# A two-layer convolution kernel: image 0's statistics partly on VectorE, ten extra matmuls at the start, and the fronts of images 1 and 2 begun two and three stages later

## The chip, the cores and the metric

The kernel runs on one core of a Trainium2 chip. The core has five engines with a queue each, worked off in order: PE (TensorE, matmuls), DVE (VectorE), ACT (ScalarE), POOL (GpSimd) and SP (SyncE, which here only issues DMAs; POOL issues DMAs too). 16 DMA engines move data between HBM and the on-chip memory SBUF; matmul results land in the accumulation memory PSUM. The metric is the device time of one execution in microseconds.

## The reference

The input x has 32 images of 256 channels and 32 x 32 pixels. Two residual layers are computed, with `_gn` a normalization over 32 groups of 8 channels:

```
x = x + L0(_gn(x));   x = x + L1(_gn(x))
L0: a = unfold(x, 3, 3); out = fq(fq(a) @ fq(weight.T)) + bias      # fq: round to 5 exponent, 10 mantissa bits
L1: y = relu(bn(w1 @ x))                                            # 256 -> 64 channels
    w = w2 @ y + b2                                                 # per pixel: 16 groups x 49 taps
    out[g, c, h, w] = sum over 49 taps k of w[g, k, h, w] * patch[g, c, k, h, w]
```

Layer 0 is a 3 x 3 convolution in float16; layer 1 is an involution: each pixel makes its own 7 x 7 filter for each of 16 groups.

## The kernel before

The 32 images go through a software pipeline. `tc.manual_schedule()` means that the written order is the order on every engine's queue. One loop runs over stages `n` from FRONT = -56 to the end; each image has 16 stages (`per`), and the main part of image b, its tap sums, starts at stage 16 b. Image b's front begins 56 stages ahead of that, so that some three and a half images are in work at a time. In a stage the loop first advances every open front by one step (each front is a generator; a `yield` ends its step), oldest image first, then issues tap sums, additions, `weights`, scatters, loads.

A front does, for one image (lines of the profile):

- statistics of layer 0: two sums of 1024 values a partition on ACT (L214, the `junk` output is thrown away, the sum is accumulated), a reduction over groups on DVE (`across`, `total`, `back`, L224 to L230), the `mean` on ACT (L235), two sums of squares on ACT (L214), the group reduction again, then `s` (square root, L245), `ve` (L247), the reciprocal `r` on DVE (L251), and `finish` on ACT: `t`, `w`, `u`, `rstd`, `off` (L256 to L267), eight small operations;
- `xq`, the normalized image in float16, by two ACT operations (L273). There is one `xq` for all images;
- the convolution: four units of 18 matmuls (`pc`, L332; 9 for each half of the input channels). After each unit DVE clamps it into `q` (L346) and adds it to x (L348), and ACT sums the new x for layer 1 (L214). Image 0 uses two PSUM buffers in turn, later images one, so the next unit waits for `q`. The units are cut into steps of 9 matmuls, 0, 9 and 0;
- the same statistics for layer 1, then `xn`, the normalized image reordered, by four ACT operations of 512 values (L273), `py` on PE (L377), `y` by two ACT operations (L388), and four times a transposition `pt` on PE (L396) with a copy to `pixels` on ACT (L400).

`weights` (eight times an image) computes the per-pixel filters on PE (`pw`, 32 matmuls, L411), and DVE adds the bias while it writes them to `w_sb` (`evict`, L435). `scatter` writes `w_sb` to HBM (`wd`, on SP, L476): a quarter of an image after its third, fifth, seventh and eighth `weights`. `load_bands` reads them back as bands (L497, 14 DMAs on POOL and 2 on SP), and `sums` multiplies bands with `pixels` on PE (`acc`, L522), which `add_windows` adds to x (L538) and `store` writes out (L543).

At the start the weights of layer 0 are loaded in two halves and clamped to float16 by `quantize_weights` on DVE (`wq`, L195), at stages FRONT + 2 and FRONT + 6.

Of the kernel before, what the change touches and what calls it, by code (L numbers as in the profile page):

```python
# [9 lines left out]
F32 = mybir.dt.float32  # L10
AF = mybir.ActivationFunctionType
ALU = mybir.AluOpType

P = 128
B, C, H, W = 32, 256, 32, 32
N = H * W
NT = 512
RT = NT // W
CH = C // P
# [6 lines left out]
GN = 8  # L26
SQ = 32
GN_EPS = 1e-5
# [44 lines left out]
FRONT = -56  # L73
LOAD = -63
LEAD = 18


@with_exitstack
def tile_quant_conv_then_involution(
# [10 lines left out]
    nc = tc.nc  # L90
# [4 lines left out]
    small = ctx.enter_context(tc.tile_pool(name="small", bufs=2))  # L95
# [5 lines left out]
    ps_m = ctx.enter_context(tc.tile_pool(name="ps_m", bufs=1, space=PSUM))  # L101

    def load_x(b):
        xt = xpool.tile([P, CH, N], F32, tag="x", name=f"x_{b}")
        for h in range(CH):
            nc.sync.dma_start(xt[:, h], x[b, h * P : (h + 1) * P])
        return xt
# [46 lines left out]
    wq = const.tile([P, CH, K0 * K0, C], F16, name="wq")  # L154
# [26 lines left out]
    for col, cols, at, n in (  # L181
# [4 lines left out]
        to = bass.AP(  # L186
            tensor=wd.tensor,
            offset=wd.offset + col * WPIX + at,
            ap=[[ROW, H], [WPIX, cols], [1, n]],
        )  # L190
        nc.sync.dma_start(to, bands[NBAND - 1][:H, 0, :n].unsqueeze(1).to_broadcast([H, cols, n]))

    def quantize_weights(kh):

        nc.vector.tensor_scalar(wq[:, kh], staged[kh], F16_MAX, -F16_MAX, ALU.min, ALU.max)  # L195
        nc.gpsimd.memset(bands[kh], 0.0)
        if kh == CH - 1:
            nc.gpsimd.memset(w_sb, 0.0)

    class GroupNorm:  # L200


        def __init__(self, b, layer):
            self.tiles = list(sums_sb[b % 2][layer])

        def begin(self, parts):
# [4 lines left out]
        def add_up(self, src, part, h, n0, n1, func, bias=0.0):  # L211
            junk = work.tile([P, N], F16, tag="junk", name="junk", bufs=1)
            i = part * CH + h
            nc.scalar.activation(  # L214
                junk[:, n0:n1], src[:, h, n0:n1], func, bias=bias, accum_out=self.sums[:, i : i + 1]
            )

        def group(self):


            if self.parts == 2:
                nc.vector.tensor_add(self.sums[:, :CH], self.sums[:, :CH], self.sums[:, CH : 2 * CH])
            across = small.tile([P, SQ], F32, tag="across", name="across")
            nc.vector.transpose(across, self.sums)  # L224
            total = small.tile([P, SQ // GN], F32, tag="total", name="total")
            nc.vector.tensor_reduce(
                total, across.rearrange("p (g r) -> p g r", r=GN), mybir.AxisListType.X, ALU.add
            )
            back = small.tile([P, SQ], F32, tag="back", name="back")
            nc.vector.transpose(back, total.unsqueeze(2).to_broadcast([P, SQ // GN, GN]))  # L230
            return back[:, :CH]
# [10 lines left out]
        def variances(self):  # L242
            pv = self.group()
            self.s = small.tile([P, CH], F32, tag="s", name="s")
            nc.scalar.activation(self.s, pv, AF.Sqrt, bias=eps, scale=1.0 / (GN * N))  # L245
            self.ve = small.tile([P, CH], F32, tag="ve", name="ve")
            nc.scalar.activation(self.ve, pv, AF.Identity, bias=eps, scale=1.0 / (GN * N))  # L247

        def scales(self):
# [3 lines left out]
        def finish(self):  # L253

            t = small.tile([P, CH], F32, tag="t", name="t")
            nc.scalar.activation(t, self.r, AF.Square)  # L256
            w = small.tile([P, CH], F32, tag="w", name="w")
            for h in range(CH):
                nc.scalar.mul(w[:, h : h + 1], t[:, h : h + 1], self.ve[:, h : h + 1])
            u = small.tile([P, CH], F32, tag="u", name="u")  # L260
            nc.scalar.activation(u, w, AF.Identity, bias=three_halves, scale=-0.5)
            self.rstd = small.tile([P, CH], F32, tag="rstd", name="rstd")
            self.off = small.tile([P, CH], F32, tag="off", name="off")
            for h in range(CH):
                one = slice(h, h + 1)
                nc.scalar.mul(self.rstd[:, one], u[:, one], self.r[:, one])
                nc.scalar.mul(self.off[:, one], self.m[:, one], self.rstd[:, one])  # L267
# [7 lines left out]
    LATER = 1  # L275

    def backwards(at):

        step, n = at.ap[-1]
        return bass.AP(tensor=at.tensor, offset=at.offset + step * (n - 1), ap=[*at.ap[:-1], [-step, n]])  # L280
# [3 lines left out]
    def front(b):  # L284


        xt = x_tiles[b]

        def stages(n):
            for _ in range(n):  # L290
                yield

        gn = GroupNorm(b, 0)
        gn.begin(1)
        for h in range(CH):
            gn.add_up(xt, 0, h, 0, N, AF.Identity)
            yield
        yield LATER
        gn.means()
# [12 lines left out]
        gn = GroupNorm(b, 1)  # L312
        gn.begin(N // NT)
        units = [(nt, mh) for nt in range(N // NT) for mh in range(CH)]
        for s in range(4 * len(units) + 2):
            u, i = divmod(s, 4)
            if u < len(units):
                nt, mh = units[u]
                if i == 0 and b == 0 and u % 2:

                    pc = ps_m.tile([P, NT], F32, tag="m", name="pc")
                elif i == 0:
                    pc = ps_c.tile([P, NT], F32, tag="pc", name="pc")
                for n in range(sum(CONV[:i]), sum(CONV[: i + 1])):
# [11 lines left out]
                        start=n == 0,  # L336
                        stop=n == CH * K0 * K0 - 1,
# [28 lines left out]
        for h in range(CH):  # L366
            yield
            to = xn[:, h].rearrange("p (k d r j) -> p d k r j", d=SIDES, r=TR, j=JC)
            at = xt[:, h].rearrange("p (k r d j) -> p d k r j", d=SIDES, r=TR, j=JC)
            gn.apply(h, [(to[:, 0], at[:, 0]), (to[:, 1], backwards(at[:, 1]))])  # L370
        yield from stages(2)

        py = ps_m.tile([P, NT], F32, tag="m", name="py")
        for kh in range(CH):
            px = xn[:, kh].rearrange("p (a i n) -> p a i n", i=2, n=2 * JC)
            for i in range(2):
# [4 lines left out]
                    start=kh == 0,  # L381
                    stop=kh == CH - 1,
                )
        to = y_sb[b % 2].rearrange("p (k r d j) -> p d k r j", k=K, d=SIDES, j=JC)
        of = py.rearrange("p (k d r j) -> p d k r j", k=K, d=SIDES, j=JC)
        for d in range(SIDES):
            at = of[:, d]
# [3 lines left out]
        for m in range(0, M, 2):  # L391
# [7 lines left out]
            to = pixels[(b * M + m) // 2 % NPIX].rearrange("p i a (v c) -> p (i a) v c", c=GC)  # L399
# [130 lines left out]
    def add_windows(b, m):  # L530

        d = m % SIDES
        to = x_tiles[b].rearrange("p h (r c) -> p h r c", c=W)
        j0 = d * (JC - PAD1)
        for g, at, top, f, l in windows(b, m):
            x_at = to[:, :, f:l, j0 : j0 + WINI]
            of = at.rearrange("p h j r -> p h r j")[:, :, f - top : l - top]
            nc.vector.tensor_tensor(x_at, of, x_at, ALU.add)  # L538

    def store(b, k):  # L540

        cols = slice(k * NT, (k + 1) * NT)
        nc.sync.dma_start(out[b].rearrange("(h p) n -> p h n", p=P)[:, :, cols], x_tiles[b][:, :, cols])  # L543
# [3 lines left out]
    per = 2 * M  # L547

    def due(n, lag):

        b, i = divmod(n - lag, per)
        return (b, i) if 0 <= b < B else (None, None)

    with tc.manual_schedule():
        fronts = {}
        for n in range(FRONT, B * per + 2):
            b, i = due(n, FRONT)
            if i == 0:
                fronts[b] = front(b)
            later = list(fronts)  # L560
            for part in range(2):
                for b in list(later):
                    got = next(fronts[b], fronts)
                    if got is fronts:
                        fronts.pop(b)
                    if got is not LATER:
                        later.remove(b)
            if n in (FRONT + CH, FRONT + CH + 4):
                quantize_weights((n - FRONT - CH) // 4)
            b, i = due(n, 0)  # L570
            if b is not None and i % 2 == 0:
                sums(b, i // 2)
            b, i = due(n, 1)
            if b is not None and i % 2 == 0:
                add_windows(b, i // 2)
                if i // 2 == M - 1:
                    store(b, 1)
                    x_tiles.pop(b)

            b, i = due(n, 2)  # L580
            if b is not None and i == 2 * (M - 1 - SIDES):
                store(b, 0)
            b, i = due(n, -LEAD)
            if b is not None and i % 2 == 0:
                weights(b, i // 2 * WR)

            for part in range(2):
                b, i = due(n, -LEAD + 1 + part)
                if b is not None and i % 2 == 0:
                    for k in range(K):  # L590
                        if i // 2 == min((k + 1) * TR // WR, H // WR - 1):
                            scatter(b, k, part)
            b, i = due(n, LOAD)
            if i == 0 and b > 1:
                x_tiles[b] = load_x(b)

            b, i = due(n, 3 - 4 * NBAND)
            if b is not None and i % 4 == 0:
                load_bands(b, i // 4)
# [38 lines left out]
```

## Time and profile before

| | |
|---|---|
| median of 3 runs | 1352.48 us (1352.35 to 1356.02) |
| the profiled execution | 1344.24 us, of which the span is 1342.5 us |
| mean granted TensorE clock | 0.982 |
| first matmul / first `py` / first `pw` | 15.24 / 50.66 / 55.66 us |
| first tap sum (`acc`) | 87.68 us |
| `py` of images 1, 2, 3, 4 | 78.53, 115.17, 155.22, 193.53 us |
| PE busy, 90 to 130 us | 40.0 of 40.0 us, DMA share 1.00 |

The profile gives, for each engine, its instructions with start, length, source line, output and inputs, and, in brackets, how long the engine was idle before and what ended that idle time. L332 is line 332 of the kernel before. `PEld` is the weight load of a matmul, which overlaps PE. "x18" at the end of a row is the number of instructions merged in it.

### The profile page before, as it was taken

What the parts mean: (1) busy time and instruction counts of PE and PEld (TensorE: products, weight loads), DVE (VectorE), ACT (ScalarE), POOL (GpSimd) and SP (SyncE); (2) the same over time, 40 slices, a digit from 0 to 9 for tenths busy, and PEclk for the clock granted to TensorE, in tenths of its full rate; (3) what the DMA queues carried; (4) which work ended last, traced back from release to release, by engine and by line L of the source; (5) the groups of instructions that cost most, each with busy time, mean ns of one, the idle gap of its engine ahead of it and who ended that gap; (6) DMA issues with size and microseconds to landing.
All of it is one profiled execution on the core that took longest, in us unless ns stands there. A gap on an engine that the chain in (4) does not pass through costs nothing.

```text
span 1342.5 us, 65799 instructions
## 1 busy us (share of the span) xinstructions
PE 1253.6 (93%) x27648; PEld 763.7 (57%) x27648; DVE 818.8 (61%) x2539; ACT 733.3 (55%) x1731; POOL 1014.4 (76%) x1818
## 2 busy tenths in 40 slices
PE   5899999999999999999999999999999999999665
PEld 2356566565555655556655556666555566556454
DVE  3466666565666665656665666766666666666442
ACT  5775656455656556556545655655556564553300
POOL 9067878777787778777778787788777877788785
PEclk9999999999999999999999999999999999999987
DMA  6089999999999999999999999999999999999995
GB/s 228 11 237 295 271 293 293 279 266 281 272 286 282 291 285 270 283 263 280 293 282 283 270 288 282 293 297 296 281 288 275 277 284 290 271 281 266 278 274 166
DMA packets 360724, 361.85 MB, mean 270 GB/s; under 512 B 75056, under 2 KB 304752, under 8 KB 359152
## 3 DMA queue, kind: packets, MB, share of 16 engines
q1 hardware_dynamic: 278512, 229.38, 56.8%
q0 software_dynamic: 81920, 128.28, 33.9%
q8 instruction: 220, 3.60, 1.1%
q14 instruction: 72, 0.59, 0.1%
HBM read 176.60 MB, written 180.76 MB: 266 GB/s over the span
## 4 chain that ended last, share of the span: by engine, by line
PE 60%; DMA 23%; POOL 7%; issue 3%; ACT 3%; DVE 2%; SPq 1%; POOLq 0%; DVEq 0%; ACTq 0%
PE pc L332 25%; PE acc L522 19%; DMA band<-wd 17%; PE pw L411 11%; POOL band L497 7%; DMA wd<-w_sb 6%; PE pt L396 3%; PE py L377 3%; ACT junk L214 1%; SPq L476 1%; DVE w_sb L435 1%; DMA x<-in_x 1%; ACT xn L273 0%; SPq L497 0%; ACT xq L273 0%
## 5 line engine op out<-in xcount | busy, mean ns | idle before, releaser
L497 POOL DMA_DIRECT2D band<-wd x1792 | 980.3, 549 | 315.7 <-DMA band<-wd 182.0
L435 DVE TENSOR_TENSOR w_sb<-pw,late_sb 128x224 f32<-128x224 f32 (+7 forms) x1280 | 330.4, 322 | 419.5 <-PE pw L411 419.2
L332 PE MATMUL pc<-xq,wq 128*128 128x496 f16 (+3 forms) x2304 | 535.2, 379 | 20.3 <-ACT xq L273 18.3
L522 PE MATMUL acc<-band,pixels 64*32 64x190 f32 (+1 forms) x16384 | 426.6, 332 | 51.8 <-DMA band<-wd 42.7
L522 PEld LDWEIGHTS acc<-band,pixels 64*32 64x32 f32 x16384 | 304.7, 107 | 159.7 <-issue 81.1
L332 PEld LDWEIGHTS <-wq 128*128 128x128 f16 x2304 | 206.7, 98 | 316.1 <-issue 102.7
L411 PE MATMUL pw<-late_sb,y 64*32 64x224 f32 (+1 forms) x8192 | 288.9, 333 | 10.8 <-issue 9.4
L538 DVE TENSOR_TENSOR x<-acc,x 128x380 f32<-128x380 f32 (+1 forms) x512 | 262.0, 512 | 32.2 <-PE acc L522 23.2
L411 PEld LDWEIGHTS pw<-late_sb,y 64*32 64x32 f32 x8192 | 186.5, 106 | 38.1 <-issue 21.0
L400 ACT COPY pixels<-pt 128x512 f32<-128x512 f32 x128 | 73.7, 576 | 228.6 <-PE pt L396 228.6
L214 ACT ACTIVATE junk<-x 128x512 f16<-128x512 f32 (+1 forms) x192 | 146.4, 763 | 14.7 <-DVE x L348 12.2
L214 ACT ACTIVATE junk<-x,mean 128x1024 f16<-128x1024 f32 x128 | 147.1, 1149 | 4.3
L245 ACT ACTIVATE s<-back,eps 128x2 f32<-128x2 f32 x64 | 18.9, 296 | 178.6 <-DVE back L230 178.6
L346 DVE TENSOR_SCALAR q<-pc 128x512 f16<-128x512 f32 x128 | 87.2, 681 | 17.6 <-PE pc L332 17.6
L273 ACT ACTIVATE xn<-x,off,rstd 128x512 f32<-128x512 f32 x128 | 96.2, 800 | 0.0
L348 DVE SCALAR_TENSOR_TENSOR x<-q,early_sb,x 128x512 f32<-128x512 f16 x128 | 94.2, 736 | 0.3
L396 PEld LDWEIGHTS pt<-ident,xn 128*128 128x128 f32 x512 | 63.9, 142 | 26.3 <-issue 2.5
L396 PE MATMUL pt<-ident,xn 128*128 128x128 f32 x512 | 78.0, 275 | 0.1
L273 ACT ACTIVATE xq<-x,off,rstd 128x1024 f16<-128x1024 f32 x64 | 75.7, 1227 | 0.0
L235 ACT ACTIVATE mean<-back 128x2 f32<-128x2 f32 x64 | 12.6, 196 | 101.4 <-DVE back L230 101.4
L377 PE MATMUL py<-xn,early_sb 128*64 128x512 f32 x256 | 62.2, 606 | 0.9 <-ACT xn L273 0.9
L224 DVE STREAM_TRANSPOSE across<-sums 128x32 f32<-128x32 f32 x128 | 26.3, 205 | 33.6 <-ACT junk L214 32.4
(40 smaller groups left out, 369.3 us busy)
## 6 DMA issues: line engine op xcount, KB each, us to landing
wd<-w_sb SPq DMA_DIRECT2D x896, 160.0 KB
band<-wd POOLq DMA_DIRECT2D x1664, 70.5 KB, 4.6
x<-in_x SPq DMA_DIRECT2D x64, 512.0 KB
out<-x SPq DMA_DIRECT2D x64, 512.0 KB
band<-wd POOLq DMA_DIRECT2D x128, 60.5 KB, 4.6
band<-wd SPq DMA_DIRECT2D x128, 50.5 KB
band<-wd SPq DMA_DIRECT2D x128, 40.5 KB
band<-in_w SPq DMA_DIRECT2D x2, 1152.0 KB
```

Of the source, the lines that this page charges most:

```text
L214: nc.scalar.activation(junk[:, n0:n1], src[:, h, n0:n1], func, bias=bias, accum_out=self.sums[:, i : i + 1])
L273: nc.scalar.activation(dst, src, AF.Identity, bias=self.off[:, one], scale=self.rstd[:, one])
L332: nc.tensor.matmul(pc.rearrange("p (r c) -> p r c", c=W)[:, r0 - nt * RT : r1 - nt * RT, c0:c1], wq[:, kh, k, mh * P : (mh + 1) * P], xq[: ...
L346: nc.vector.tensor_scalar(q, pc, F16_MAX, -F16_MAX, ALU.min, ALU.max)
L348: nc.vector.scalar_tensor_tensor(xt[:, mh, cols], q, bias_sb[:, mh : mh + 1], xt[:, mh, cols], ALU.add, ALU.add)
L377: nc.tensor.matmul(py[i * CR : (i + 1) * CR], w1_sb[:, kh, :], px[:, :, i], start=kh == 0, stop=kh == CH - 1,)
L396: nc.tensor.transpose(pt[:, i, h * P : (h + 1) * P], xn[:, h, (m + i) * P : (m + i + 1) * P], ident)
L411: nc.tensor.matmul(pws[i][t * TW : (t + 1) * TW, : dj.stop - dj.start, r], y_sb[b % 2][half, (r0 // 2 + r) * W : (r0 // 2 + r + 1) * W], w ...
L435: nc.vector.tensor_tensor(to, of[:, :, d0:d1], bias[:, :, d0:d1], ALU.add)
L497: queue.dma_start(to, src)
L522: nc.tensor.matmul(at[t * TW : (t + 1) * TW, h, :, f - top : l - top], px[p, a, v * GC : v * GC + TW], of[:, :, a, f - top : l - top, v], ...
L538: nc.vector.tensor_tensor(x_at, of, x_at, ALU.add)
```

## The change

Four things are edited.

- Image 0's statistics: the second half's sum of layer 0 is a DVE reduction; in both layers `ve` and `finish` of image 0 are small DVE operations on both halves at once (five after the reciprocal, in place of eight on ACT). Of image 0's four `xn` operations two go to DVE.
- Ten matmuls of 512 columns on the first half of the clamped weights are issued right after that half is clamped; their result is not used. The second half is clamped at stage FRONT + 7 in place of FRONT + 6.
- The front of image 1 is held for its first two stages, that of image 2 for its first three (`HELD`).
- From its stage 16 on (`CATCH`), every second stage, a held front gets one additional step, two times for image 1 and three times for image 2, so that it is level with the others again before the tap sums of image 0 begin.

```diff
+WARM = 10
+HELD = {1: 2, 2: 3}
+CATCH = 16

+    def warm_up():
+
+        pc = ps_m.tile([P, NT], F32, tag="m", name="warm_pc")
+        for _ in range(WARM):
+            nc.tensor.matmul(pc, wq[:, 0, 0, :P], wq[:, 0, 1:3], start=True, stop=True)

         def __init__(self, b, layer):
+            self.first = b == 0

+        def add_up_by_vector(self, src, h):
+            nc.vector.tensor_reduce(self.sums[:, h : h + 1], src[:, h], mybir.AxisListType.X, ALU.add)

             self.ve = small.tile([P, CH], F32, tag="ve", name="ve")
+            if self.first:
+                nc.vector.tensor_scalar(self.ve, pv, 1.0 / (GN * N), GN_EPS, ALU.mult, ALU.add)
+                return
             nc.scalar.activation(self.ve, pv, AF.Identity, bias=eps, scale=1.0 / (GN * N))

             t = small.tile([P, CH], F32, tag="t", name="t")
+            if self.first:
+                self.rstd = small.tile([P, CH], F32, tag="rstd", name="rstd")
+                self.off = small.tile([P, CH], F32, tag="off", name="off")
+                nc.vector.tensor_mul(t, self.r, self.r)
+                nc.vector.tensor_mul(t, t, self.ve)
+                nc.vector.tensor_scalar(t, t, -0.5, 1.5, ALU.mult, ALU.add)
+                nc.vector.tensor_mul(self.rstd, t, self.r)
+                nc.vector.tensor_mul(self.off, self.m, self.rstd)
+                return
             nc.scalar.activation(t, self.r, AF.Square)

         for h in range(CH):
-            gn.add_up(xt, 0, h, 0, N, AF.Identity)
+            if b == 0 and h:
+                gn.add_up_by_vector(xt, h)
+            else:
+                gn.add_up(xt, 0, h, 0, N, AF.Identity)
             yield

-            gn.apply(h, [(to[:, 0], at[:, 0]), (to[:, 1], backwards(at[:, 1]))])
+            if b == 0:
+                one = slice(h, h + 1)
+                nc.vector.tensor_scalar(
+                    to[:, 0], at[:, 0], gn.rstd[:, one], gn.off[:, one], ALU.mult, ALU.add
+                )
+            else:
+                gn.apply(h, [(to[:, 0], at[:, 0])])
+            gn.apply(h, [(to[:, 1], backwards(at[:, 1]))])

-            later = list(fronts)
-            for part in range(2):
-                for b in list(later):
-                    got = next(fronts[b], fronts)
-                    if got is fronts:
-                        fronts.pop(b)
-                    if got is not LATER:
-                        later.remove(b)
-            if n in (FRONT + CH, FRONT + CH + 4):
-                quantize_weights((n - FRONT - CH) // 4)
+            steps = [[b for b in fronts if not 0 <= n - FRONT - b * per < HELD.get(b, 0)]]
+            for b, held in HELD.items():
+                if n - FRONT - b * per in range(CATCH, CATCH + 2 * held, 2):
+                    steps.append([b])
+            for later in steps:
+                for part in range(2):
+                    for b in list(later):
+                        got = next(fronts[b], fronts)
+                        if got is fronts:
+                            fronts.pop(b)
+                        if got is not LATER:
+                            later.remove(b)
+            if n == FRONT + CH:
+                quantize_weights(0)
+                warm_up()
+            if n == FRONT + CH + 5:
+                quantize_weights(1)
```

## The prediction

> **What bounds the kernel now.** I read the page first (busy shares, slices), then the chain that ended last over the first 120 us, then PE's timeline there, then stretches of the DMA share. The change edits image 0's statistics and the places of the fronts of images 1 and 2, so only the ramp can move; the order of work from image 0's first `sums` on is the same in both programs.
>
> ```profile
> PE 1253.6 (93%) x27648; PEld 763.7 (57%) x27648; DVE 818.8 (61%) x2539; ACT 733.3 (55%) x1731; POOL 1014.4 (76%) x1818
> ...
> PE   5899999999999999999999999999999999999665
> ...
> DMA  6089999999999999999999999999999999999995
> ```
>
> PE and the 16 DMA engines are both at 9 tenths from about 80 us to 1240 us. Nothing there has slack to win back a late start, so the ramp's length is paid in full, or nearly. I follow it to one mark: the first `acc` matmul (`sums`, L522) of image 0.
>
> ```profile
> 14.05 1.14 ACT xq L273
> 15.24 13.83 PE pc L332 x54
> ...
> 34.30 1.23 ACT xq L273
> 35.57 5.67 PE pc L332 x18
> ...
> 58.69 1.14 ACT xq L273
> 59.88 2.07 PE pc L332 x9
> ...
> 85.74 2.01 PE pc L332 x9
> 87.75 1.34 PE acc L522 x44
> ```
>
> Columns: start, length, work. The chain enters PE three times from an ACT `xq`: images 0, 1 and 2. The mark stands at 87.68. PE's timeline shows how it waits for them:
>
> ```profile
> 35.57 5.65 PE L332 MATMUL pc<-xq,wq 128*128 128x512 f16 x18 [2.71 <-ACT xq L273]
> 42.00 3.97 PE L332 MATMUL pc<-xq,wq 128*128 128x512 f16 x18 [0.78 <-DVE q L346]
> 46.76 3.97 PE L332 MATMUL pc<-xq,wq 128*128 128x512 f16 x18 [0.78 <-DVE q L346]
> 50.66 1.94 PE L377 MATMUL py<-xn,early_sb 128*64 128x512 f32 x8
> 52.53 2.08 PE L332 MATMUL pc<-xq,wq 128*128 128x512 f16 x9
> 55.66 0.98 PE L411 MATMUL pw<-late_sb,y 64*32 64x224 f32 x32 [1.05 <-ACT y L388]
> ...
> 59.88 2.07 PE L332 MATMUL pc<-xq,wq 128*128 128x512 f16 x9 [0.32 <-ACT xq L273]
> ```
>
> From the first `pw` (55.66) to the mark PE idles only some 1.5 us: those 32 us are work. A change can shorten them by little, and lengthens them by every new idle.
>
> ```profile
> 15.24:19.77 4.53, 4.53 (x11) 1.57 (x11) 1.27 (x8) 1.17 (x2) 4.53 (x1) 1.00 1.08 372
> 19.77:32.90 13.13, 13.09 (x62) 5.98 (x61) 5.54 (x13) 7.99 (x20) 13.13 (x3) 1.00 0.15 60
> 35.50:40.10 4.60, 4.53 (x14) 1.76 (x14) 0.77 (x4) 3.59 (x8) 0.00 (x0) 0.65 0.02 4
> ```
>
> First column after the length: PE busy and its matmuls. The first 11 take 0.41 us each, the next 62 0.21: 2.2 us lost to a slow start, though the clock column (third from the end) says 1.00. After the 2.71 us idle at 32.86 the granted clock falls to 0.65, and the unit takes 5.65 instead of 3.97.
>
> **The change, part by part.**
>
> Image 0's statistics. The second half's sum goes from ACT (1.06, ready 1.15 after its start at 5.72) to a DVE reduction of 1024 values. No row has it; by 0.79 ns a value (`wq` quantization, 1.82 for 2304) it is 0.8, by 1.46 (L348, 0.75 for 512) 1.5. It starts when its half of x lands, at 5.72 or earlier, so the sum is ready between 1.1 earlier and 0.35 later; I take no gain. An earlier one could not pass 0.3, since the quantization holds DVE until 10.28 and the next group stands at 10.60. Nine ACT operations from `ve` to `off` become six DVE ones, `ve` beside the square root: after the reciprocal (11.81) ACT needed until 14.05, DVE needs five at the 0.19 pitch of the `bn` operations, until 12.8. So `xq` is ready 1.2 us earlier, at 14.0. The second quantization follows on DVE, 12.8 to 14.6; its cover is the first nine matmuls, which do not read it.
>
> Warm-up. Ten matmuls of 512 columns start when the first quantization ends (10.3), at the slow 0.41 to 0.43 pitch: done at 14.6. They stand ahead of the convolution on PE and take back 0.6 of the 1.2. The slow phase was 4.5 us at 15.24; ten cover 4.2 of it. So image 0's 72 matmuls run at 0.21 from 14.6, and units of 3.81 end at 18.6, 22.4, 26.2 and 30.0, where before they ended at 21.47, 25.28, 29.09 and 32.90: 2.9 us ahead.
>
> [...]
>
> Image 1's front, two stages late. In the built order ACT now does both `junk` sums of image 0's units 0 and 1 before image 1's two sums. The second waits for unit 1 (22.4, q 0.73, x 0.75: 23.9), so image 1's sums start at 24.7, where they started at 23.85 with units 2.9 later: ACT idles 3 us instead of filling. From there by the rows of before: sums ready 27.1, `back` 27.8, mean, squares 28.1 to 30.6, `back` 31.4, square root. DVE has unit 3's q (0.69) ahead of the reciprocal: 32.3. ACT's finish 2.10, a `junk` 0.65, `xq` 1.23 + 0.04: PE starts image 1 at 36.4, not 35.57. It has then idled 6.3 us. What a cold start costs lies between 1.7 (5.65 - 3.97) and 3.4 (all 18 at 0.41 less 3.97); I take 2.2, the row of the start, also after a long idle. Unit 0 ends at 42.6 (before 41.22).
>
> Units 1 and 2 follow (3.97 and 0.75 each; the latter is the q wait) and stand ahead of `py` on PE: `py` at 52.0 (before 50.66). Image 0's own scales are earlier and half on DVE (its `xn` parts at 0.4 to 0.75 each lie under unit 1), which is worth nothing while PE is at image 1. One gain: `y` no longer stands behind image 2's squares on ACT (54.61) but follows `py`, at 54.0. `pw` 1 then waits only for nine matmuls: 55.8 against 55.66. The 2.9 us are gone.
>
> Image 2's front, three stages late. Its sums stood at 46.5 and 48.9, its `xq` was ready at 59.83. Now the first stands behind a `junk` that waits for image 1's unit 1 (about 50), the second behind `y`: 54.9. `back` 56.8; squares to 59.6; `back` 60.3, square root. DVE now has that group ahead of `pw` 2's four evictions (1.20) and image 1's last x (0.75) ahead of the reciprocal: 62.5. A `junk` waits for the same x, then finish 2.11, `xq` 1.23: 66.3, which is 6.5 later. PE has meanwhile done `pw` 2, a `pt` and `pw` 3, which waited 1.4 for those evictions, and a second `pt`; it idles from 63.1 to 66.3. The second half of `xq` stands behind the squares of image 1 (2.5) and a `pixels` copy (0.5) on ACT: 70.8. So image 2's first unit ends at 72.8.
>
> Its second unit, on the same PSUM buffer, waits for its q, and that stands on DVE behind `pw` 5's evictions: 72.8 + 1.1 + 1.2 + 0.73 = 75.9. Then without gaps but one q wait: `pc` 2.01, `pw` 0.91, `pc` 2.01, q 0.8, `pc` 2.01, `pw` 0.91, `py` 1.87, `pc` 2.01, `pw` 0.91, `pc` 2.01, `pw` 0.91, `pc` 2.01 = 18.4: the mark at 94.2 instead of 87.68. **Plus 6.5 us.** A slow clock at 66.3 would add between 0 (the wait for the second half covers it) and 0.7; I take 0.
>
> Queues. SP and POOL hold the same issues in the same order. The first scatter follows `pw` 3's evictions (63.9 against 64.6), the second `pw` 5's (75.1 against 71.7), the third and fourth `pw` 7's and 8's (86 and 91 against 80.9 and 83.9). No band becomes the last wait for the mark, but transfers queue less at it. The first wait for a band after it was 1.02 us:
>
> ```profile
> 146.46 1.62 PE L522 MATMUL acc<-band,pixels 64*32 64x190 f32 x62 [1.02 <-DMA band<-wd]
> ```
>
> A later PE no longer waits there. I give back this one wait: 6.5 - 1.0 = 5.5 us. The profiled execution took 1344.24 us (span 1342.5 and 1.7 around it), so by its own sum 1349.7; the median shown is 1352.48, 8.2 above it, and the difference goes on top: 1358.0.
>
> **Rivals.** (1) The transfers set the pace. For it: DMA share 0.94 to 1.00 in every stretch from 90 us, and the first scatter 0.7 us earlier. Then PE's lag is taken up by waits for bands: -0.7 (1351.8) if the first scatter counts, up to +3.4 if the second does. It decides once waits for bands before 1240 us exceed the lag; against it, PE did not wait at all from 88 to 145 us. This one is not slower by more than can be told. (2) The head start survives: if image 1 were ready by 30.0, the 2.9 us reached the mark, 1349.6. Against it: image 1's sums cannot pass the `junk` of unit 1. (3) The cold clock is worse: 3.4 for 2.2 at image 1 and 0.7 at image 2: 6.5 + 1.2 + 0.7 = +8.4, 1360.9. (4) The warm-up does nothing: the convolution's own 2.2 us slow phase stays, image 0 is 0.7 ahead instead of 2.9, and the sums of image 1, hung on unit 1, start 2.2 later; +7.7, 1360.2.
>
> **How the numbers follow.** A measurement tells 0.3% (4.1 us). Forecast and (4) together 0.70, from +3.5 to +8; (3) 0.08; (1) 0.14; (2) 0.08. Of the first 0.05 lies under 4.1 us, (1) is all within the bound, (2) is within it or, with every slow matmul gone besides (-2.9 - 2.2), beyond. Slower 0.73, same 0.22, faster 0.05. The range runs from rival (1)'s early end to rival (3) with 1 us over it: 1351.5 to 1362. The likeliest case's own range is 1356 to 1361.
>
> **What would show it.** Right: first convolution matmul of image 0 near 14.6 directly behind the warm-up, its last near 30; image 1's first near 36.4 after over 5 us of idle, at a low clock; `pw` 1 within 1 us of 55.66; a PE idle of about 3 us before image 2's first matmul near 66; the first `acc` near 94. Wrong: image 1's first matmul before 34, or image 2's before 62, or a first `acc` at or before 88; or the first `acc` late and the end not, which is rival (1).

## The result, and the profile after

The changed kernel takes 1370.16 us (1369.4 to 1372.35, 4 executions), the kernel before 1353.9 us (4 executions, three of them those of the table ahead of the prediction): a ratio of 1.0123, 95% interval 1.008 to 1.0166, slower by 16.3 us. The forecast had the side right and the size at a third: 5.5 us. A second comparison, with 10 and 31 executions on one chip (run e5 below), gave 1.0059 (1.0031 to 1.0088), 1355.71 against 1346.76 us. Ratios and intervals leave out executions more than 1.5% above the fastest of their kernel, so a ratio can differ from that of the medians, and e8's profiled execution is one of those left out.

The page of the changed kernel is that of before with a longer ramp. These are its busy shares and two rows of its slices:

```profile
PE 1256.1 (92%) x27658; PEld 761.3 (56%) x27658; DVE 828.7 (61%) x2554; ACT 728.0 (53%) x1709; POOL 1013.2 (74%) x1818
...
PE   5789999999999999999999999999998999999655
...
DMA  6079999999999999999999999999999999999995
```

Nothing in it names a cause. PE's timeline of the ramp does (start, length, engine, line, work, count, idle before and what ended it; the convolution is now L360, `py` L412, `pw` L446, `acc` L557):

```profile
10.34 4.45 PE L207 MATMUL warm_pc<-wq 128*128 128x512 f16 x10 [10.34 <-DVE wq L198]
14.75 2.26 PE L360 MATMUL pc<-xq,wq 128*128 128x512 f16 x9
20.22 13.51 PE L360 MATMUL pc<-xq,wq 128*128 128x496 f16 x63 [3.21 <-DVE bn_ve L175]
39.95 6.89 PE L360 MATMUL pc<-xq,wq 128*128 128x512 f16 x18 [6.22 <-ACT xq L298]
...
56.27 1.94 PE L412 MATMUL py<-xn,early_sb 128*64 128x512 f32 x8
...
60.15 0.97 PE L446 MATMUL pw<-late_sb,y 64*32 64x224 f32 x32
...
70.44 3.42 PE L360 MATMUL pc<-xq,wq 128*128 128x512 f16 x9 [3.05 <-ACT xq L298]
...
98.58 1.41 PE L557 MATMUL acc<-band,pixels 64*32 64x133 f32 x60
```

The warm-up and the first nine matmuls stand where they were forecast (10.3 and 14.6). Then there is a hole that was not: 3.21 us before the tenth matmul. After it the forecast's steps come in order, each 3.5 to 4.4 us late: image 1 at 39.95 for 36.4, the first `pw` at 60.15 for 55.8, image 2 at 70.44 for 66.3, the first `acc` at 98.58 for 94.2. Before, that mark stood at 87.68: the ramp has grown by 10.9 us.

The hole is the second quantization (the row names `bn_ve`, which stands directly behind it on DVE). The same stretch of the changed kernel on DVE and POOL:

```profile
8.68 1.60 DVE L198 TENSOR_SCALAR wq<-band 128x2304 f16<-128x2304 f32 x1 [0.97 <-DMA band<-in_w]
...
12.28 0.75 DVE L277 TENSOR_SCALAR t<-t 128x2 f32<-128x2 f32 x1
...
12.96 5.99 POOL L199 MEMSET band<- 128x7056 f32 x1
13.34 6.82 DVE L198 TENSOR_SCALAR wq<-band 128x2304 f16<-128x2304 f32 x1
...
20.22 5.98 POOL L199 MEMSET band<- 128x7056 f32 x1 [1.27 <-DVE bn_ve L175]
```

and in the kernel before:

```profile
8.46 1.82 DVE L195 TENSOR_SCALAR wq<-band 128x2304 f16<-128x2304 f32 x1 [0.80 <-DMA band<-in_w]
...
11.72 1.80 DVE L195 TENSOR_SCALAR wq<-band 128x2304 f16<-128x2304 f32 x1
...
14.15 11.89 POOL L196 MEMSET band<- 128x7056 f32 x2
```

The same operation took 1.80 and 6.82 us. In the changed kernel it is issued at 13.34, 0.4 us after POOL began to clear the first staging band, and ends 1.2 us after that memset does (18.95). The two touch different tiles: the memset clears the first band, the quantization reads the second. Even `t`, an operation on two values, took 0.75 us, where it took 0.17 in e2 and e8: it ends at 13.03, the last memset of `pixels` at 13.02.

The clock is the other difference. Of the stretches of the changed kernel (columns: stretch, its length, busy time and count of PE, weight loads, DVE, ACT, POOL, then granted clock, DMA share, GB/s) two ran at a granted clock of 0.57 and 0.59, image 1's first unit and the start of image 2's:

```profile
17.00:20.20 3.20, 0.01 (x1) 0.00 (x0) 3.20 (x2) 0.00 (x0) 1.95 (x1) 1.00 1.03 411
20.20:33.80 13.60, 13.51 (x63) 6.18 (x64) 6.11 (x18) 5.95 (x13) 13.58 (x2) 1.00 0.12 48
39.90:46.90 7.00, 6.89 (x18) 2.45 (x18) 0.97 (x6) 4.00 (x7) 0.00 (x0) 0.57 0.01 2
70.40:73.80 3.40, 3.36 (x12) 1.10 (x12) 0.00 (x0) 3.34 (x7) 0.00 (x0) 0.59 0.92 240
```

### The profile page after: what moved, and what is told of

Same layout as the page of the kernel before. It is cut to its first block, busy times and chain, and to the rows that moved or that the text cites. A ratio compares the mean times of both kernels' runs of the same rounds, so it can differ in the third digit from the quotient of the medians.

```text
span 1367.9 us, 65815 instructions
## 1 busy us (share of the span) xinstructions
PE 1256.1 (92%) x27658; PEld 761.3 (56%) x27658; DVE 828.7 (61%) x2554; ACT 728.0 (53%) x1709; POOL 1013.2 (74%) x1818
## 3 DMA queue, kind: packets, MB, share of 16 engines
q1 hardware_dynamic: 278512, 229.38, 55.8%
## 4 chain that ended last, share of the span: by engine, by line
PE 57%; DMA 23%; POOL 7%; issue 5%; DVE 3%; SPq 1%; ACT 1%; POOLq 0%; DVEq 0%; ACTq 0%
PE pc L360 24%; PE acc L557 18%; DMA band<-wd 18%; PE pw L446 10%; POOL band L532 7%; DMA wd<-w_sb 5%; PE pt L431 3%; PE py L412 2%; DVE w_sb L470 1%; SPq L511 1%; ACT junk L224 0%; DVE x L573 0%; DVE q L374 0%; DMA out<-x 0%; SPq L532 0%
## 5 line engine op out<-in xcount | busy, mean ns | idle before, releaser
L360 PE MATMUL pc<-xq,wq 128*128 128x496 f16 (+3 forms) x2304 | 535.7, 379 | 19.0 <-ACT xq L298 9.3
L557 PE MATMUL acc<-band,pixels 64*32 64x190 f32 (+1 forms) x16384 | 425.5, 331 | 62.5 <-DMA band<-wd 38.9
L557 PEld LDWEIGHTS acc<-band,pixels 64*32 64x32 f32 x16384 | 302.6, 107 | 172.8 <-issue 94.3
L360 PEld LDWEIGHTS <-wq 128*128 128x128 f16 x2304 | 206.7, 98 | 318.3 <-issue 110.9
L446 PE MATMUL pw<-late_sb,y 64*32 64x224 f32 (+1 forms) x8192 | 284.8, 329 | 15.0 <-issue 14.3
L446 PEld LDWEIGHTS pw<-late_sb,y 64*32 64x32 f32 x8192 | 185.1, 105 | 39.2 <-issue 24.7
L224 ACT ACTIVATE junk<-x 128x1024 f16<-128x1024 f32 (+1 forms) x191 | 145.4, 761 | 20.8 <-DVE x L376 13.6
L412 PE MATMUL py<-xn,early_sb 128*64 128x512 f32 x256 | 62.0, 605 | 0.0
L423 ACT ACTIVATE y<-py,bn_shift,bn_scale 128x256 f32<-128x256 f32 x64 | 32.3, 555 | 20.9 <-PE py L412 20.7
```

Source lines behind the costliest of these rows:

```text
L224: nc.scalar.activation(junk[:, n0:n1], src[:, h, n0:n1], func, bias=bias, accum_out=self.sums[:, i : i + 1])
L360: nc.tensor.matmul(pc.rearrange("p (r c) -> p r c", c=W)[:, r0 - nt * RT : r1 - nt * RT, c0:c1], wq[:, kh, k, mh * P : (mh + 1) * P], xq[: ...
L412: nc.tensor.matmul(py[i * CR : (i + 1) * CR], w1_sb[:, kh, :], px[:, :, i], start=kh == 0, stop=kh == CH - 1,)
L446: nc.tensor.matmul(pws[i][t * TW : (t + 1) * TW, : dj.stop - dj.start, r], y_sb[b % 2][half, (r0 // 2 + r) * W : (r0 // 2 + r + 1) * W], w ...
L557: nc.tensor.matmul(at[t * TW : (t + 1) * TW, h, :, f - top : l - top], px[p, a, v * GC : v * GC + TW], of[:, :, a, f - top : l - top, v], ...
```

## The experiments

Twelve runs in three groups, each group on a chip of its own, beside executions of the kernel before: e1 to e4 (25 executions of before, median 1347.13 us), e5 to e8 (31, 1346.76) and e9 to e12 (35, 1346.42). Marks and medians of different groups are thus compared across chips. "Rest" is the median less the first `acc` of the one profiled execution.

| run | first `acc` | median us | rest | ratio to before (95%) |
|---|---|---|---|---|
| before (mark from its one trace) | 87.68 | 1347 | 1259 | |
| e1 memsets after the quantizations | 95.59 | 1353.12 | 1257.5 | 1.0056 (1.0023 to 1.0089) |
| e2 no holds | 83.63 | 1348.21 | 1264.6 | 1.0015 (0.9978 to 1.0051) |
| e3 both | 82.59 | 1343.0 | 1260.4 | 0.9974 (0.9936 to 1.0011) |
| e4 holds alone | 98.42 | 1357.61 | 1259.2 | 1.0121 (1.004 to 1.0201) |
| e5 changed kernel again | 96.87 | 1355.71 | 1258.8 | 1.0059 (1.0031 to 1.0088) |
| e6 e3 + hold of image 1 | 88.29 | 1348.73 | 1260.4 | 1.0021 (0.9995 to 1.0048) |
| e7 e3 + hold of image 2 | 91.35 | 1350.49 | 1259.1 | 1.0006 (0.9971 to 1.004) |
| e8 e3 + another memset first | 94.64 | 1356.54 | 1261.9 | 1.0036 (0.9994 to 1.0078) |
| e9 e3 again | 84.58 | 1337.58 | 1253.0 | 0.9954 (0.9924 to 0.9984) |
| e10 e3 without the ten matmuls | 85.08 | 1341.08 | 1256.0 | 0.997 (0.994 to 1.0) |
| e11 e3, image 0 on ACT | 85.79 | 1343.77 | 1258.0 | 0.9977 (0.9938 to 1.0015) |
| e12 quantization one stage earlier | 96.65 | 1356.72 | 1260.1 | 1.0058 (1.0023 to 1.0092) |

Theory P was that DVE's quantization and POOL's memset exclude each other; theory H, that the held fronts make images 1 and 2 late as the prediction worked out; R0, that the time differs by the shift of the first `acc` and nothing else.

**e1, the memsets after the quantizations.** Edit, against the changed kernel:

```diff
-        nc.gpsimd.memset(bands[kh], 0.0)
         if kh == CH - 1:
+            for band in reversed(bands[:CH]):
+                nc.gpsimd.memset(band, 0.0)
             nc.gpsimd.memset(w_sb, 0.0)
```

> The changed kernel with one edit: POOL clears both weight staging bands only after the second quantization, instead of the first band right after the first quantization. Theory P (POOL and DVE exclude each other): in the changed kernel the second quantization (6.82 us from 13.34) waited for POOL's 5.99 us memset that had begun at 12.96; here it takes under 2 us, image 0's convolution runs without a gap from 14.7 to about 30.2, image 1's first matmul stands near 36.4 (39.95 in the changed kernel) and the first acc near 94.3 (98.6), so the time is about 4.3 us under the changed kernel, 12 over before. Rival D (the second half of the weights lands late or the DMA traffic slows DVE): the quantization still ends near 20 and nothing moves.

PE's timeline of e1 (lines one higher than in the changed kernel), then its quantization and the memsets behind it:

```profile
14.75 15.40 PE L361 MATMUL pc<-xq,wq 128*128 128x512 f16 x72
36.37 6.22 PE L361 MATMUL pc<-xq,wq 128*128 128x512 f16 x18 [6.21 <-ACT xq L299]
...
55.90 0.97 PE L447 MATMUL pw<-late_sb,y 64*32 64x224 f32 x32
...
66.19 3.92 PE L361 MATMUL pc<-xq,wq 128*128 128x512 f16 x9 [3.05 <-ACT xq L299]
70.04 1.73 PE L447 MATMUL pw<-late_sb,y 64*32 64x224 f32 x32
...
95.59 1.43 PE L558 MATMUL acc<-band,pixels 64*32 64x133 f32 x59
```

```profile
13.34 1.35 DVE L198 TENSOR_SCALAR wq<-band 128x2304 f16<-128x2304 f32 x1
...
14.76 11.90 POOL L201 MEMSET band<- 128x7056 f32 x2 [1.74 <-DVE bn_ve L175]
```

Issued at the same 13.34, the quantization takes 1.35 us, and image 0's 72 matmuls run without a gap. Image 1's first matmul is back by 3.6 us, at the 36.4 of the forecast; the first `pw` stands at 55.90 (forecast 55.8), image 2 at 66.19 (66.3). P holds, rival D falls. The mark is 95.59, not 94.3: image 2's nine matmuls took 3.92 instead of 2.08 and the next `pw` 1.73 instead of 0.97, at a granted clock of 0.50 from 66 to 70 us. The time came out 6 us over before, not the 12 expected, a figure that carried the 16.3 of the first comparison.

**e8, another memset.** Is it the tile or the engine? Edit, against e3:

```diff
-        if kh == CH - 1:
+        if kh == 0:
+            nc.gpsimd.memset(w_sb, 0.0)
+        else:
             for band in reversed(bands[:CH]):
                 nc.gpsimd.memset(band, 0.0)
-            nc.gpsimd.memset(w_sb, 0.0)
```

> The kernel of e3 with POOL's memset of w_sb (8.63 us), a tile that the quantization does not touch, put ahead of the second quantization. Theory P (the two engines exclude each other, whatever the tile): the quantization waits for its end near 21.6 and ends near 22.8, image 0's convolution has a gap of 6 us, the first acc is near 88.5. Rival T (it was a dependence on the band tiles): the quantization takes 1.4 us as in e3 and the first acc stays at 82.6.

DVE and POOL of e8:

```profile
7.66 4.13 POOL L150 MEMSET pixels<- 128x768 f32 x6
...
8.74 12.84 DVE L198 TENSOR_SCALAR wq<-band 128x2304 f16<-128x2304 f32 x1 [1.05 <-DMA band<-in_w]
...
11.74 8.63 POOL L200 MEMSET w_sb<- 128x10240 f32 x1
...
23.59 1.35 DVE L198 TENSOR_SCALAR wq<-band 128x2304 f16<-128x2304 f32 x1
```

The expectation named the wrong victim and the right mechanism. The first quantization, issued at 8.74, waited through the remaining memsets of `pixels` and the whole memset of `w_sb`, which it does not touch, and ended 1.2 us after it, at 21.6; the second then took 1.35. So it is the memset on the other engine, whatever its tile, not a dependence on the bands: rival T falls. In the changed kernel, e4, e5 and e8 alike, a held quantization ends 1.2 us after the last memset that it met. It holds the other way too: where a quantization got in among the six memsets of `pixels`, one of these took 1.94 us in place of 0.73 (before, the changed kernel), and all six 5.36 and 5.38 us (e1, e2); in e4 and e8, where none got in, they took 4.13. The first `acc` went to 94.64, 12.1 later than in e3, not 6, since the warm-up and the statistics' second half waited too.

**e2 and e3, no holds.** Edit of e2, against the changed kernel; e3 has e1's edit as well:

```diff
-HELD = {1: 2, 2: 3}
+HELD = {}
```

> The changed kernel with no held fronts; the DVE statistics, the ten matmuls and the later quantization stay. Theory H (the holds make image 1 and 2 late): image 1's first matmul near 36.3, the first pw near 56, image 2's first matmul near 60.5, the first acc near 88.5, the time within 2 us of before, 14 to 16 under the changed kernel. Rival Q (the quantization stall alone is the loss): the first acc stays at 94 or later and the time 6 or more over before.

> The changed kernel without holds and with the POOL memsets after the second quantization: both suspected costs gone. If P and H are both right, image 0's convolution ends near 30, image 1 starts near 32.6, the first acc stands near 84.7, 3 us ahead of before, and the time is 3 us under before. If one of them is wrong, the first acc is at 88 or later.

The first `acc` falls to 83.63 and 82.59. e2 came out better than expected because there the quantization got in ahead of the memset (issued at 12.67, memset at 12.99, no gap in image 0's 72 matmuls): two traces of the same queues on two sides of a race of a few tenths of a microsecond. H holds: without the holds the ramp is 3 to 5 us shorter than before (e2, e3, e9), with them 8 to 11 longer (e1, e4, e5, e12 and the changed kernel's trace). In time e2 is not to be told from before; e3 needed more executions (e9).

**e4, the holds alone**, in the kernel before.

```diff
+HELD = {1: 2, 2: 3}
+CATCH = 16
...
-            later = list(fronts)
...
+            steps = [[b for b in fronts if not 0 <= n - FRONT - b * per < HELD.get(b, 0)]]
...
```

> The kernel before with the held fronts and their catch-up alone. Theory H: image 1's first matmul near 39.3, the first acc near 97.5, the time about 10 us over before. Rival (the holds are harmless or help when image 0 is slow): the first acc at 88 or earlier. In all four runs, theory R0 says that the time less the first acc is one figure for all (1266 from before's median, 1271.6 from the changed kernel's); rival R1 says that a kernel with holds loses more after the first acc too.

Mark 98.42 and 10.5 us more, near the expectation, but by chance in part: here the race was lost twice, in code of image 0 that the edit does not touch (L197 is L195 of before).

```profile
8.75 4.25 DVE L197 TENSOR_SCALAR wq<-band 128x2304 f16<-128x2304 f32 x1 [1.21 <-DMA band<-in_w]
...
14.03 6.22 DVE L197 TENSOR_SCALAR wq<-band 128x2304 f16<-128x2304 f32 x1
```

So the kernel before has this hazard too; in its own trace the quantization got in between two memsets. "Holds cost 10" cannot be read off e4; e6 and e7 price them without the race.

**e6 and e7, one hold at a time**, in e3: `HELD = {1: 2}` and `HELD = {2: 3}`.

> The kernel of e3 (no holds, memsets after) with image 1 alone held, two stages. From e1 and e3: image 1's first matmul goes from 33.7 to about 36.4 with a cold start after 6 us of idle, the first pw from 51.0 to about 56, the first acc from 82.6 to 87 to 88: plus 5. Rival: it costs nothing alone, and image 2's hold makes the whole 13 us between e3 and e1.

> The kernel of e3 with image 2 alone held, three stages. The first pw stays near 51, PE then waits for image 2's xq, the first acc goes from 82.6 to about 90.6: plus 8. The two single holds should add up to the 13.0 us between the first acc of e1 and of e3.

From e3's 82.59, image 1's hold adds 5.7 (expected 5) and image 2's 8.8 (expected 8). Together 14.5; e1 less e3 is 13.0. e9, e3 again, has its mark at 84.58, so such sums are good to 2 us, mostly through image 1's first unit, which took 3.97 us in e3 and 5.50 in e9. Against e9 the two holds add 3.7 and 6.8, and e1 less e9 is 11.0. The waits stand where the prediction put them: image 1's 6 us idle in e6, and in e7 image 2's, behind a `pw` that waits for its evictions:

```profile
36.50 6.84 PE L361 MATMUL pc<-xq,wq 128*128 128x512 f16 x18 [6.21 <-ACT xq L299]
```

```profile
57.78 1.56 PE L447 MATMUL pw<-late_sb,y 64*32 64x224 f32 x32 [0.61 <-DVE w_sb L471]
62.98 2.73 PE L361 MATMUL pc<-xq,wq 128*128 128x512 f16 x9 [3.06 <-ACT xq L299]
```

In time the two single holds cannot be told from before (1.0021 and 1.0006). The interval of e6 lies above that of e9, that of e7 overlaps it.

**e5, the changed kernel again.** No edit.

> The changed kernel once more, beside before on one chip, with more executions. If the loss is the ramp alone (theory R0): if the second quantization again waits for POOL (ends near 20), the first acc is near 98.6 and the time 10 to 11 us over before; if this time it gets in ahead of the memset, the first acc is near 95.6 and the time 6 to 8 over. Rival R1 (the part after the first acc is itself longer in this program): 14 us or more over before.

The quantization was held again, 6.82 us from 13.34. Image 1's unit took 5.68 us for 6.89, the mark is 96.87, 9.2 over before's, and the time 9 us over before in medians. R0 holds here and R1, a longer rest, does not: the rest is 1258.8 against 1259.

**e9, the better version again.** e3 with more executions.

> The kernel of e3 (no holds, POOL's memsets after the second quantization) with more executions: its first acc stood 5.1 us ahead of before's, and by theory R0 (the loss or gain is the shift of the first acc) the time is 5 us under before, a ratio of 0.996. Rival: the part after it takes the gain back, ratio 1.

0.9954 (0.9924 to 0.9984), 1337.58 against 1346.42 us: faster than both kernels. The mark is 3.1 us ahead of before's; the other 5.7 of the 8.8 us between the medians it does not explain. The interval allows 2.2 to 10.2 us, and e3's own comparison gave 0.9974, so the size of the gain is known no better than that.

**e10 and e11, what the other two parts are worth.** e10 deletes the call of `warm_up()` in e3; e11 sets `self.first = False` and puts the second sum and the `xn` parts back on ACT.

> The kernel of e3 without the ten matmuls. If they only move the slow phase away: the convolution starts at 14.7, its first 11 matmuls take 0.41 us, unit 0 ends 1.5 us later than in e3, image 1's sums follow it, the first acc near 84.1, 1.5 later. Rival: they are worth nothing, first acc at 82.6 or earlier.

> The kernel of e3 with image 0's statistics and scales back on ACT. Behind ten matmuls that end near 15 the earlier xq has nothing to gain: xq ready near 15.2, the convolution starts within 0.6 us of e3's, and the first acc stands at 82.6 to 83.5. Rival: the DVE statistics carry a gain of 1.2 us or more, first acc at 84 or later.

Without the ten matmuls the convolution begins at 14.75 and its 72 matmuls take 17.03 us instead of 15.70 and 16.16 (e3, e9); the mark is 0.5 to 2.5 later than theirs. The expected 1.5 lies inside, but two traces of one kernel differ by as much (e3 and e9). With image 0 on ACT the mark is 1.2 to 3.2 later, against an expectation of 0 to 0.9: the rival was nearer. The convolution starts within 0.3 of e3's as I said, but `y` stands behind image 2's squares on ACT again, and PE waits 1.05 us for it before the first `pw`, which it does not in e3. It is the gain that the prediction had named and this expectation forgot.

**e12, the second quantization one stage earlier**, in the changed kernel:

```diff
-            if n == FRONT + CH + 5:
+            if n == FRONT + CH + 4:
```

> The changed kernel (holds and all) with the second quantization back at stage FRONT + 6. It is then issued near 11.8, ahead of the band memset, and waits at most for one memset of pixels: it ends near 14, the convolution has no gap, starts 0.5 to 1.2 us later since the scales follow the quantization on DVE, and the first acc is near 96.5, 2 us under the first trace of the changed kernel. Rival: with the clearing of the band still right behind the first quantization, the second waits here too, acc at 98 or later.

Issued at 11.98 it took 1.55 us; no gap; the convolution started at 15.95; mark 96.65, as expected. So in this trace the earlier stage kept it ahead of the memset of the band (14.16). It is no guarantee: e4 has the same stage, and there the quantization took 6.22 us. In time e12 and e5 cannot be told apart, as their marks (96.65, 96.87) say.

## Why the prediction was right and wrong

**Right: the direction and its mechanism.** The holds make image 1 and image 2 late by the queues' order, and the head start of image 0 is gone by the first `pw`. With the race taken out (e1) the steps land on the forecast: image 0 from 14.75 (14.6), image 1 at 36.37 (36.4), the first `pw` at 55.90 (55.8), image 2 at 66.19 (66.3). That they land within 0.2 us is partly luck: in e1 the warm-up started 0.7 us later than forecast (11.02) and ran 0.8 faster (3.62 us), and image 1's cold start, 2.25 us there at a granted clock of 0.50, measured 1.7 to 2.9 in the traces with its hold. Rival (2), a head start that survives, is what e3 shows once the holds are gone, and only then.

**Wrong: "The second quantization follows on DVE, 12.8 to 14.6; its cover is the first nine matmuls".** I took 1.82 us from the trace of before and asked who waits for it, not what it waits for. It took 6.82 us, ended at 20.2, and the nine matmuls covered 2.3 of that. Image 1's first matmul is 3.6 us later for it (39.95 against 36.37 in e1, and the same in e5). The marks differ by less, 3.0 between the changed kernel's trace and e1 and 1.3 between e5 and e1, because image 1's first unit, image 2's first nine matmuls and the `pw` behind them took 11.87 us in e1 together (6.22, 3.92, 1.73), 11.28 in the changed kernel (6.89, 3.42, 0.97) and 8.71 in e5 (5.68, 2.06, 0.97), which lost 0.9 again by waiting, 0.48 of it for `xq`. The same wait held `t` by 0.6 us, so `xq` was ready at 14.7 for 14.0, which the warm-up's end at 14.8 hid. The warning stood in the trace of before: L195 took 1.82 and 1.80 us, and POOL cleared tiles throughout (6.55 us of memsets of `pixels` from 7.65); the same operation ran in 1.35 in e1, where POOL was idle from 13.02 to 14.76. Why the two operations exclude each other no run shows.

**Wrong by its size: the slow clock at image 2.** "A slow clock at 66.3 would add between 0 (the wait for the second half covers it) and 0.7; I take 0." From image 2's first matmul to the mark the forecast has 27.9 us. e4 and e5, where that unit was not slow (nine matmuls in 2.07 and 2.06 us), took 27.6, the changed kernel (3.42) 28.1, e1 and e12 (3.92 in both) 29.4 and 29.3. So the cover is too small: in e1 the `pw` behind the nine matmuls ran slow too (1.73 for 0.91 to 0.97), and I had priced the nine alone. Image 1's cold start, taken at 2.2, measured 2.9 in the changed kernel, 1.7 in e5 and 2.25 in e1. Rival (3), a worse cold clock, was right in part; its 8.4 leaves out the 1.0 given back, which the sums of the forecast and of rival (4) hold.

**Not borne out: "I give back this one wait: 6.5 - 1.0".** The wait at 146 us did go; the first of 0.5 us or more for a band now comes at 207 us, with 1.06 us. But no run shows a gain from it: the rests scatter by 11 us around one figure, and 1.0 us cannot be told in them. Rival (1), the transfers set the pace, falls with it: a mark later by 9.2 costs 9 us.

**Right within 0.8 us: the warm-up takes the slow phase.** The forecast let image 0's 72 matmuls run at 0.21 us each from the first on. Behind the ten matmuls they took 15.40 us in e1 and e12, the least in any trace, and 15.70 and 16.16 in e3 and e9, that is 0.3 and 0.8 more; before they took 17.63, and in e10, without the ten, 17.03. In the changed kernel the first nine took 2.26 us for 2.08. What makes these times vary no run shows.

**Where the 16.3 us are.** 10.9 are in the ramp: by the forecast's terms 6.5, the held quantization 3.6, and 0.8 besides, most of it image 1's cold start (2.9 for 2.2, at a granted clock of 0.57). The other 5.4 lie after the first `acc`, where both programs do the same. So the forecast's 5.5 missed 10.8: 3.6, 0.8, the 1.0 given back, and these 5.4. In e1 to e12 no such part appears: the rests lie between 1253 and 1264.6 us, with and without holds, around before's 1259, and a line through the twelve shifts of mark and median has the slope 1.03. e5 is the same program as the changed kernel. Its profiled execution spends 1258.2 us behind the first `acc` (1355.07 less 96.87), that of the changed kernel's first trace 1271.1 (1369.71 less 98.58), and before's 1256.6. So the 5.4 are not in every execution of the program, and e5's interval, 4.2 to 11.9 us over before, does not reach 16.3. Whether they are scatter or came from that comparison's chip stays open: it had four executions on each side, and one kernel's executions differ by 16 to 21 us (before: 1338.98 to 1354.8 beside e5, 1333.8 to 1355.0 beside e1). The 9 us of e5 agree with the ramp alone.

## What to carry to other kernels

When an operation is moved in time, look at what runs on the neighbouring engine at its new place: the same quantization took 1.35 us with POOL idle (e1), 1.80 among the memsets of `pixels` (before) and 6.82 beside a 5.99 us memset (the changed kernel), and the 1.80 for 1.35 showed a wait before anything was moved. Holding work back paid nothing here, because the engine that it freed had nothing else to do: ACT idled 3 us (3.07 in the changed kernel), image 1's first matmul came 2.8 us later (e6 against e3) and the first `acc` 5.7. And in this ramp, which ends in a loop with PE and DMA at 9 tenths, one mark (the first `acc`) told the change of the time more sharply than the time itself: two traces of one kernel (e3, e9) differ by 2 us in it, the executions of before by 16 to 21 us.

## What was not expected of the hardware

- DVE's float32 to float16 quantization of 2304 values, 1.35 us alone, waited for the memsets of POOL that it met, whatever tile they cleared (`pixels`, a band, `w_sb`), up to 12.84 us in all (e8). The reduction of 1024 values (1.22 us, inside the 5.97 us memset) and the clamp `q` from PSUM (0.69 us, beside the 8.63 us memset) did not, in the changed kernel.
- Between two memsets that follow each other without a pause DVE's first quantization was let in in 12 of 14 traces, but in e4 and e8 not once until POOL had nothing ready (it then idled 1.27 and 4.64 us). Traces with the same code at the start so differ: image 0's convolution ended at 30.6 us in e2 and at 33.7 in the changed kernel. That one program's executions differ by this is likely, but the two traces of the changed kernel do not show it: both were held.
- The rest after the first `acc` stayed within 1253 to 1264.6 us while the mark moved by 16 us: within that scatter, the ramp was paid in full.
